# Depthwise convolution of q and k on TensorE: tiles of 64x64 replaced by tiles of 32x32, and another layout of the spilled q and k

## The chip, the core and the metric

The kernel runs on one NeuronCore of a Trainium2 chip. The metric is device time in microseconds (us) of one execution, given as the median of several runs. The core has a matrix engine (TensorE, "PE" in the profile, with its weight loads shown apart as "PEld"), a vector engine (VectorE, "DVE"), a scalar engine (ScalarE, "ACT"), GpSimd ("POOL"), and SyncE ("SP"), which here only issues DMA transfers. All arrays are float32 in this part of the kernel.

## The reference, cut to what matters

The input is x of shape (4, 192, 128, 128). Layer 0 is a channel attention; layer 1 is a dilated neighbourhood attention that takes its result and that the change does not touch.

```python
# layer 0, with 8 heads of ch = 24 channels
qkv = dwconv3x3(conv1x1(x, w_qkv), w_dw)          # 4*192 channels, 3x3 depthwise, zero padding
q, k, v, l = jnp.split(qkv, 4, axis=1)
q, k, v = (heads(q), heads(k), heads(v))          # (4, 8, 24, 128*128)
q = q / jnp.maximum(jnp.linalg.norm(q, axis=-1, keepdims=True), EPS)
k = k / jnp.maximum(jnp.linalg.norm(k, axis=-1, keepdims=True), EPS)
attn = jnp.einsum('bhcn,bhdn->bhcd', q, k) * temperature[None]
attn = softmax(attn, axis=-1)                     # only 24x24 for each head and image
out = jnp.einsum('bhcd,bhdn->bhcn', attn, v)
out = conv1x1(L + out + x, w_proj) + L            # L: a gate from the pooled l
```

So q and k, 192 channels each, are needed only for a 24x24 product and for the sums of their squares.

## The kernel before, in words

The kernel has three stages, which follow one another with some overlap.

**project** (about 0 to 820 us) computes the 1x1 convolution in 64 steps of four image rows, two images at a time. The columns for q and k, not yet convolved, are copied from PSUM by ScalarE (line 438) and written to a DRAM scratch tensor `qk_dram` by `qk_store` (lines 440 to 445, on SP's queue). Its shape is `[2 * C, H, B, W]`: by channel, then row, then image. One channel is 256 KiB in one piece. v is convolved in this stage on VectorE, ScalarE and GpSimd.

**channel_attention** (about 817 to 1598 us; line 657) runs over 8 heads. For each head, `convolved` runs once for q and once for k. It works in groups of four channels:

- SP loads a tile `u` (128 partitions, each holding image rows; 4 buffers) by four transfers of 64 partitions each (line 696), and two band matrices for each of two channels into `band` (line 693; 3 buffers).
- The 128 image rows of a channel are two strips of 64. The 3x3 convolution is a matrix product over rows: for each horizontal tap dx, a 64x64 band matrix holds the three vertical taps, and the shift in dx is a shift of the columns of the moving operand. Two channels share the 64x64 quarters of the array: channel e of the pair and strip r use the partitions `(r + e) % 2 * 64`. These are the matmuls of line 714.
- GpSimd copies the band from one half of the partitions to the other (line 701) and zeroes one of its columns (line 704).
- ScalarE copies the finished 128x512 channel from PSUM into `full` (tile name `conv`, line 723), and VectorE takes its statistics with four bn_stats (line 727), from PSUM but for the first set.

A band in a strip of 64 rows cuts off the taps across the strip border. What is missing in the two rows at the border (63 and 64), is computed by `cut_rows` (line 740): four rows, 24 channels each, are loaded (line 748), multiplied by `cuttaps` (tile `pcut`, line 756), copied (line 768), transposed on TensorE (line 771) and added: to the squares on VectorE and, as four small matmuls (line 801), to the product. For this to be sound, one column of each band is zeroed, so that the border rows get nothing from the strips.

`products` (line 781) is the 24x24 product for four images: 128 matmuls with a contraction over 128 rows, `gram` (line 786), followed by small sums (lines 801 to 818). `finish` (line 825) does the norm, softmax and the mix with the projection in pieces; `step()` runs one piece after each group of four channels.

The order on each engine in this stage is chosen by the framework's own scheduler, which may let TensorE run ahead into the next head's convolution while VectorE ends the small sums. In the other two stages the order is written out by the class `Schedule`.

**second_pass** (from about 1598 us) is layer 1.

A tensor in the trace takes its name from the variable; a float32 matmul shows as two MATMUL and two LDWEIGHTS instructions.

Of the kernel before, what the change touches and what calls it, by code (L numbers as in the profile page):

```python
# [7 lines left out]
F32 = mybir.dt.float32  # L8
# [23 lines left out]
QR = 28  # L32

# [280 lines left out]
def channel_attention_then_dilated_attention(ctx: ExitStack, tc: tile.TileContext, d, out: bass.AP):  # L314
# [16 lines left out]
    qk_dram = dram.tile([2 * C, H, B, W], F32, tag="qk_dram", name="qk_dram")  # L331
# [5 lines left out]
    with ExitStack() as early:  # L337
        band_p, u_p = (early.enter_context(tc.tile_pool(name=n, bufs=k)) for n, k in (("pab", 3), ("pau", 4)))
# [50 lines left out]
def plan_projection(nc, stage, x, wx, wx2, dwv, vboth, ring, sums, qk_dram, v_dram, v2_dram):  # L389
# [50 lines left out]
    def qk_store(n, mt):  # L440
        im0, rows = place(n)
        nc.sync.dma_start(
            qk_dram[mt * 128 : (mt + 1) * 128, rows, im0 : im0 + 2, :].rearrange("c h b w -> c h (b w)"),
            tiles.pop(("us", n, mt)).rearrange("p h b w -> p h (b w)"),
        )
# [211 lines left out]
def channel_attention(tc, d, load, qk_dram, mix1, mix2, band_p, u_p, gates):  # L657
# [7 lines left out]
    with ExitStack() as ctx:  # L665
# [3 lines left out]
        cut_p = ctx.enter_context(tc.tile_pool(name="pac", bufs=1))  # L669
        st = ctx.enter_context(tc.tile_pool(name="pas", bufs=1))  # L670
# [4 lines left out]

        logits = fin.tile([CH0, B, HEADS0, CH0], F32, tag="logits", name="logits")
        nq = fin.tile([CH0, B, HEADS0], F32, tag="nq", name="nq")
        nk = fin.tile([CH0, B, HEADS0, CH0], F32, tag="nk", name="nk")
        half = CH0 // 2

# [3 lines left out]
        def convolved(hd, which, pool):  # L684
            c0 = which * C + hd * CH0
            full = pool.tile([128, B, W // 4, CH0, 4], F32, tag="conv", name=f"conv{which}_{hd}")
            stats = st.tile([128, B, CH0, 6], F32, tag=f"stats{which}", name=f"stats{which}_{hd}")
            for c2 in range(0, half, 2):
                band = band_p.tile([128, 2, 2, 3, G], F32, tag="band", name=f"band{which}_{hd}_{c2}")
                u = u_p.tile([128, 2, 2, B * W], F32, tag="u", name=f"u{which}_{hd}_{c2}")  # L690
                for e in range(2):
                    first = c0 + e * half + c2
                    nc.sync.dma_start(band[HALVES[e], e], d["bands"][:, first : first + 2])
                    for r in range(2):
                        to = (r + e) % 2 * G
                        nc.sync.dma_start(
                            u[to : to + G, e],
                            qk_dram[first : first + 2, r * G : (r + 1) * G].rearrange("c h b w -> h c (b w)"),
                        )
                for e in range(2):  # L700
                    nc.gpsimd.tensor_copy(band[HALVES[1 - e], e], band[HALVES[e], e])  # L701
                    for r in range(2):
                        cut = G - 1 - r * (G - 1)
                        nc.gpsimd.memset(band[HALVES[(r + e) % 2], e, :, :, cut : cut + 1], 0.0)
                for c in range(2):
                    pcs = [
                        ps_c.tile([128, B, W], F32, tag="pc", name=f"pc{which}_{hd}_{c2}_{c}_{e}") for e in range(2)
                    ]
                    for dx in (1, 0, 2):
                        to, of = shifted(dx)  # L710
                        for e in range(2):
                            for r in range(2):
                                at = slice((r + e) % 2 * G, (r + e) % 2 * G + G)
                                nc.tensor.matmul(  # L714
                                    pcs[e][r * G : (r + 1) * G, :, to],
                                    band[at, e, c, dx, :],
                                    u[at, e, c, :].rearrange("p (b w) -> p b w", w=W)[:, :, of],
                                    start=dx == 1,
                                    stop=dx == 2,
                                )  # L720
                    for e in range(2):
                        ch = e * half + c2 + c
                        nc.scalar.copy(full[:, :, :, ch, :], pcs[e].rearrange("p b (v w) -> p b v w", w=4))  # L723
                        for b in range(B):

                            of = pcs[e][:, b, :] if hd or which else full[:, b, :, ch, :]
                            nc.vector.bn_stats(stats[:, b, ch, :], of)  # L727
                step()

            flat = stats.rearrange("p b c s -> p (b c) s")  # L730
            sq = st.tile([128, B, CH0], F32, tag=f"sq{which}", name=f"sq{which}_{hd}")
            sqf = sq.rearrange("p b c -> p (b c)")
            nc.vector.tensor_mul(flat[:, :, 1:5:3], flat[:, :, 1:5:3], flat[:, :, 1:5:3])
            nc.vector.tensor_add(sqf, flat[:, :, 1], flat[:, :, 4])
            nc.vector.tensor_scalar_mul(sqf, sqf, float(W // 2))
            nc.vector.tensor_add(sqf, sqf, flat[:, :, 2])
            nc.vector.tensor_add(sqf, sqf, flat[:, :, 5])
            return full, sq

        def cut_rows(hd, sums):  # L740


            pcut = ps_c.tile([128, B, W], F32, tag="pc", name=f"pcut{hd}")
            for which in range(2):
                c0 = which * C + hd * CH0
                u = cut_p.tile([4 * CH0, B * W], F32, tag=f"u{which}", name=f"cut{which}_{hd}")
                for r in range(4):
                    nc.sync.dma_start(
                        u[r * CH0 : (r + 1) * CH0],
                        qk_dram[c0 : c0 + CH0, G - 2 + r].rearrange("c b w -> c (b w)"),  # L750
                    )
                taps = cut_p.tile([4 * CH0, 3, 2 * CH0], F32, tag=f"taps{which}", name=f"cuttaps{which}_{hd}")
                nc.sync.dma_start(taps, d["cuttaps"][:, which * HEADS0 + hd])
                for dx in (1, 0, 2):
                    to, of = shifted(dx)
                    nc.tensor.matmul(
                        pcut[which * G : which * G + 2 * CH0, :, to],
                        taps[:, dx, :],
                        u.rearrange("p (b w) -> p b w", w=W)[:, :, of],
                        start=dx == 1,  # L760
                        stop=dx == 2,
                    )
            s_cut = cut_p.tile([128, B, W], F32, tag="s_cut", name=f"s_cut{hd}")
            if hd == 0:
                nc.gpsimd.memset(s_cut, 0.0)
# [3 lines left out]
            turned = ps_c.tile([128, B, 128], F32, tag="pc", name=f"turned{hd}")  # L769
            for b in range(B):  # L770
                nc.tensor.transpose(turned[:, b, :], s_cut[:, b, :], ident)
            cut = cut_p.tile([128, B, 2, G], F32, tag="cut", name=f"cutT{hd}")
            nc.scalar.copy(cut.rearrange("p b k c -> p b (k c)"), turned)
            square = cut_p.tile([128, B, 2, G], F32, tag="square", name=f"square{hd}")
# [4 lines left out]
            return cut  # L779

        def products(hd, q, sq, k, sk, cut):
            gram = ps_g.tile([HALF, B, HALF], F32, tag="gram", name=f"gram{hd}")
            for b in range(B):
                for v in range(W // 4):
                    four = lambda a: a[:, b, v].rearrange("p c w -> p (c w)")
                    nc.tensor.matmul(gram[:, b, :], four(q), four(k), start=v == 0, stop=v == W // 4 - 1)  # L786

            kept = st.tile([HALF, B, CH0, 4], F32, tag="kept", name=f"kept{hd}")
# [11 lines left out]
            for b in range(B):  # L800
                nc.tensor.matmul(extra[:, b, :], cut[:, b, 0, :two], cut[:, b, 1, :two], start=True, stop=True)
# [23 lines left out]
        def finish(hd):  # L825
# [22 lines left out]
            mixed = fin.tile([CH0, B, C], F32, tag="mixed", name=f"mixed{hd}")  # L848
            low = min(max(128 - hd * CH0, 0), CH0)
            for b in range(0, B, 2):  # L850
                pm = ps_g.tile([HALF, B, HALF], F32, tag="gram", name=f"pm{hd}_{b}")
# [3 lines left out]
                nc.vector.tensor_copy(mixed[:, b : b + 2, :], two)  # L855
            for b in range(B):
                if low:
                    nc.sync.dma_start(mix1[b][hd * CH0 : hd * CH0 + low], mixed[:low, b, :])
                if low < CH0:
                    at = G + hd * CH0 + low - 128  # L860
                    nc.sync.dma_start(mix2[b][at : at + CH0 - low], mixed[low:, b, :])
# [10 lines left out]
        for hd in range(HEADS0):  # L872
            q, sq = convolved(hd, 0, q_p)
            if hd == 0:
                same, same_row, fold, fold_rows, ones, ident, wph, tempr = (
                    load(wts, n) for n in "same same_row fold fold_rows ones ident wph temp".split()
                )
            k, sk = convolved(hd, 1, k_p)
            products(hd, q, sq, k, sk, cut_rows(hd, (sq, sk)))
            pending.append(finish(hd))  # L880
        while pending:
            step()
# [540 lines left out]
def _laid_out(inputs):  # L1423
# [33 lines left out]
    bands = np.zeros((G, 2 * C, 3, G), dw.dtype)  # L1457
    taps = dw[: 2 * C].reshape(2 * C, 3, 3)
    cuttaps = np.zeros((4, CH0, 2 * HEADS0, 3, 2, CH0), dw.dtype)
    for dy in range(3):  # L1460
        o = np.arange(max(0, 1 - dy), min(G, G + 1 - dy))
# [59 lines left out]
```

## Time and profile before

| | |
|---|---|
| time, median of 3 runs | 4362.7 us (4361.42 to 4363.07) |
| profiled execution, its span | 4359.7 us |
| profiled execution, its own time | not given apart from the span; the median lies 3.0 us above the span |
| channel attention, from the first conv matmul to the hand-over to layer 1 | 816.9 to 1598.2 us |
| one head in the middle of that stage | 960.36 to 1053.30 us: 92.94 us |
| busy in that head | PE 92.94, DVE 51.20, ACT 31.31, POOL 17.05 us; DMA 0.78, 171 GB/s |
| first head, 842 to 907 us | PE 64.93 of 65.00 us; DMA 0.96, 214 GB/s |

"Busy" is the time in which at least one instruction of the engine ran. The DMA share is the mean over the 16 DMA engines. The chain of waits is the list of work that ended last, followed back from the end; in the channel attention it runs almost wholly over TensorE. Matmul records overlap: the mean duration of one says how long it was in the array, not how often one starts.

### The profile page before, as it was taken

The page shows a single profiled execution, that of the slowest core. Times are in us where ns is not written, and L with a number is a line of the kernel's source. Part 1 is how long each engine was busy: PE and PEld are TensorE (multiplying, and loading weights), DVE is VectorE, ACT ScalarE, POOL GpSimd, SP SyncE. Part 2 cuts the span into 40 slices and gives each one's busy share as a digit, 9 for nine tenths or more (in the row PEclk, how much of TensorE's full clock was granted, in tenths as well). Part 3 has the DMA queues.
Part 4 walks back from the last instruction along what each step waited for, and adds up shares of the span by engine and source line. Part 5 has one row for each costly group of instructions (what it writes and reads, how often), then busy time and mean ns, then how long its engine had stood idle before and what let it go on. Part 6 is the DMA issues. An engine that isn't in the chain of part 4 may idle for free.

```text
span 4359.7 us, 64790 instructions
## 1 busy us (share of the span) xinstructions
PE 4248.5 (97%) x20736; PEld 1639.7 (38%) x20736; DVE 3805.5 (87%) x5492; ACT 2602.5 (60%) x4858; POOL 3316.0 (76%) x3407
## 2 busy tenths in 40 slices
PE   8999999899999989999999999999999999999996
PEld 3333333344554543333333333333333333333321
DVE  6999999855545547999999999999999999999996
ACT  6999999633323347565655655656656566566531
POOL 5888888611111114999999999999999999999998
PEclk9999999999999999999999999999999999999997
DMA  8887898778867757666666666656566566565521
GB/s 261 266 269 251 271 280 269 205 171 177 178 145 161 171 118 157 134 129 129 134 124 131 135 125 130 134 122 136 124 130 129 129 134 127 128 135 124 115 53 32
DMA packets 507362, 684.14 MB, mean 157 GB/s; under 512 B 139584, under 2 KB 321292, under 8 KB 507024
## 3 DMA queue, kind: packets, MB, share of 16 engines
q1 hardware_dynamic: 469136, 513.27, 44.9%
q0 software_dynamic: 37888, 166.74, 21.1%
q8 instruction: 167, 2.74, 0.3%
q14 instruction: 171, 1.40, 0.1%
HBM read 286.04 MB, written 201.33 MB: 112 GB/s over the span
## 4 chain that ended last, share of the span: by engine, by line
PE 78%; DVE 14%; issue 4%; POOL 2%; DMA 1%; ACT 1%; SPq 0%; DVEq 0%; POOLq 0%; ACTq 0%
PE pc L714 12%; PE sc L1179 9%; PE ex L1301 8%; PE ph L946 7%; PE pu L413 7%; PE pkv L1100 5%; DVE term L1307 4%; PE gram L786 4%; PE pkv L1103 4%; PE q L1160 4%; PE q L1157 4%; PE pu L418 3%; DVE prod L1168 3%; PE pu L564 2%; PE po L1323 2%
## 5 line engine op out<-in xcount | busy, mean ns | idle before, releaser
L1310 POOL TENSOR_TENSOR acc<-acc,term 128x512 f32<-128x512 f32 x1536 | 2035.8, 1331 | 132.1 <-DVE term L1307 45.1
L1307 DVE TENSOR_TENSOR term<-ex,vring 128x512 f32<-128x512 f32 (+2 forms) x1596 | 996.9, 660 | 55.4 <-PE ex L1301 40.6
L1168 DVE TENSOR_TENSOR prod<-q,kring 128x1536 f32<-128x1536 f32 (+1 forms) x600 | 1005.3, 1684 | 15.9 <-PE q L1157 7.7
L490 POOL TENSOR_TENSOR v_True<-v_True,side 128x512 f32<-128x512 f32 (+1 forms) x512 | 643.8, 1270 | 128.9 <-ACT side L479 99.1
L467 DVE SCALAR_TENSOR_TENSOR pa<-vboth,dwv,pa 128x1024 f32<-128x1024 f32 (+1 forms) x448 | 574.3, 1282 | 39.3 <-ACT pa L460 12.9
L1301 PE MATMUL ex<-e_sb,spread 108*128 108x512 bf16 x1728 | 567.5, 387 | 37.0 <-DVE term L1307 31.3
L701 POOL COPY band<-band 64x384 f32<-64x384 f32 x192 | 96.4, 502 | 569.8 <-DMA band<-in_bands 413.2
L714 PE MATMUL pc<-u,band 64*64 64x508 f32 (+1 forms) x4608 | 523.1, 592 | 3.1 <-ACT vboth L449 2.2
L1113 ACT COPY kring<-pkv 64x512 f32<-64x512 f32 x384 | 223.5, 582 | 417.9 <-PE pkv L1103 412.4
L998 DVE SCALAR_TENSOR_TENSOR pa<-hboth,posw,pa 128x1024 f32<-128x1024 f32 (+1 forms) x320 | 407.8, 1274 | 38.0 <-ACT pa L986 19.1
L1179 PE MATMUL sc<-prod,pick 128*32 128x512 f32 x3456 | 428.5, 598 | 1.8 <-DVE prod L1168 1.8
L727 DVE BATCH_NORM_STATS2 stats<-pc 128x6 f32<-128x128 f32 x1440 | 303.3, 283 | 141.0 <-ACT conv L723 140.7
L723 ACT COPY conv<-pc 128x512 f32<-128x512 f32 x384 | 211.5, 587 | 300.5 <-PE pc L714 288.1
L1301 PEld LDWEIGHTS <-spread 108*128 108x128 bf16 x1728 | 133.3, 97 | 647.0 <-issue 628.6
L1100 PE MATMUL pkv<-y,wkv 128*128 128x512 f32 x768 | 364.5, 596 | 10.7 <-DMA y<-moved 10.5
L413 PE MATMUL pu<-xt,wx 128*128 128x512 f32 x768 | 358.4, 610 | 16.6 <-ACT vboth L449 8.6
L946 PE MATMUL ph<-xv,mix 128*64 128x512 f32 (+1 forms) x1024 | 373.5, 594 | 0.5 <-DMA mix<-mixed 0.5
L479 ACT ACTIVATE side<-ring,dwv 128x512 f32<-128x512 f32 (+1 forms) x512 | 347.7, 723 | 27.2 <-POOL v_True L490 23.2
L1326 ACT COPY o<-po 128x512 f32<-128x512 f32 x192 | 106.3, 588 | 430.9 <-PE po L1323 227.0
L1030 ACT ACTIVATE side<-hring,posw 128x512 f32<-128x512 f32 (+1 forms) x512 | 340.9, 710 | 7.8 <-DMA side<-side 5.8
L714 PEld LDWEIGHTS pc<-u,band 64*64 64x64 f32 x4608 | 186.7, 134 | 311.2 <-issue 292.0
L1113 ACT COPY vring<-pkv 64x512 f32<-64x512 f32 x384 | 224.1, 584 | 46.1 <-PE pkv L1103 32.8
(167 smaller groups left out, 6052.7 us busy)
## 6 DMA issues: line engine op xcount, KB each, us to landing
qk_dram<-us SPq DMA_DIRECT2D x192, 512.0 KB
u<-qk_dram SPq DMA_DIRECT2D x384, 256.0 KB
side<-side POOLq DMA_DIRECT2D x124, 768.0 KB, 6.9
xt<-in_x SPq DMA_DIRECT2D x64, 512.0 KB
v_dram<-v_False SPq DMA_DIRECT2D x64, 512.0 KB
xv<-in_x SPq DMA_DIRECT2D x128, 256.0 KB
xv<-v_dram SPq DMA_DIRECT2D x128, 256.0 KB
y<-moved POOLq DMA_DIRECT2D x64, 512.0 KB, 5.2
```

The lines of the kernel that those rows point to most:

```text
L413: mm(pu, wx[:, mt * 128 : (mt + 1) * 128], tiles["xt", n][:, im, :], start=True, stop=False)
L467: nc.vector.scalar_tensor_tensor(by_row(to[:, o : o + length]), by_row(vboth[:, at : at + length, :, t % 3 : t % 3 + W]), dwv[:, 0, t : t ...
L490: nc.gpsimd.tensor_add(v[:, rows, :], v[:, rows, :], z[:, rows, :])
L714: nc.tensor.matmul(pcs[e][r * G : (r + 1) * G, :, to], band[at, e, c, dx, :], u[at, e, c, :].rearrange("p (b w) -> p b w", w=W)[:, :, of], ...
L946: mm(to, w[:, cols], tiles["xv", n, j, im], start=j == 0, stop=j == 2)
L1100: mm(rows3(tile_of("pc", key)), w, tiles["y", n, im], start=True, stop=False)
L1113: nc.scalar.copy(rows[HALVES[im], :, pad : pad + W], rows3(tiles["pkv", n, pair, im])[HALVES[e]])
L1168: nc.vector.tensor_mul(to[:, :, px].rearrange("p t (r w) -> p t r w", w=W), q.unsqueeze(1).to_broadcast([128, 3, *q.shape[1:]]), three,)
L1179: mm(sc[quad * 32 : (quad + 1) * 32, :], pick[:, QR - 4 * row : QR - 4 * row + 32], tiles["prod", n, k // NT, k % NT // 3][:, k % 3, :], s ...
L1301: mm(rows3(tile_of("ex", ("ex", n, g, t))), spread[:, t, :], e_sb, start=True, stop=True)
L1307: nc.vector.tensor_mul(rows3(to[:, px]), rows3(ex[:, px]), win)
L1310: nc.gpsimd.tensor_add(tiles["acc", n, g], tiles["acc", n, g], tiles.pop(("term", n, g, t)))
```

## The change

The strips are 32 rows high instead of 64, so there are four of them, and four channels share the array: channel e and strip r use the partitions `(r + e) % 4 * 32`. A channel now needs 4 strips times 3 taps of 32x32 matmuls. A group is eight channels, with a `u` tile of twice the size and 2 buffers instead of 4; the bands are 32x32, loaded once into `few` (32 partitions, one buffer) and copied by GpSimd into all four strips of one of two fixed `band` tiles, in twelve copies for a group. There are three inner borders (after rows 31, 63, 95), each with its own cut convolution. `qk_dram` becomes `[H, 2 * C, B, W]`: by row, then channel. bn_stats always reads `full`. On TensorE the order in this stage is now the program's own: channels are interleaved by the key `0.75 * n + k`.

```diff
-    qk_dram = dram.tile([2 * C, H, B, W], F32, tag="qk_dram", name="qk_dram")
+    qk_dram = dram.tile([H, 2 * C, B, W], F32, tag="qk_dram", name="qk_dram")
...
-        band_p, u_p = (... for n, k in (("pab", 3), ("pau", 4)))
+        band_p, u_p = (... for n, k in (("pab", 1), ("pau", 2)))
...
-            qk_dram[mt * 128 : (mt + 1) * 128, rows, im0 : im0 + 2, :].rearrange("c h b w -> c h (b w)"),
+            qk_dram[rows, mt * 128 : (mt + 1) * 128, im0 : im0 + 2, :].rearrange("h c b w -> c h (b w)"),
...
+        bands = [band_p.tile([128, 4, 2, 3, STRIP], F32, tag=f"band{k}", name=f"band{k}") for k in range(2)]
+        for band in bands:
+            nc.gpsimd.memset(band, 0.0)
...
+        def loaded(hd, which, j):
+            c0 = which * C + hd * CH0 + j
+            few = few_p.tile([STRIP, 4, 2, 3, STRIP], F32, tag="few", name=f"few{which}_{hd}_{j}")
+            nc.sync.dma_start(few..., d["bands"]...)
+            u = u_p.tile([128, 4, 2, B * W], F32, tag="u", name=f"u{which}_{hd}_{j}")
+            for e in range(4):
+                turn = e * STRIP
+                for to, of in ((slice(turn, 128), slice(0, 128 - turn)), (slice(0, turn), slice(128 - turn, 128))):
+                    if of.start == of.stop:
+                        continue
+                    first = c0 + e * (CH0 // 4)
+                    nc.sync.dma_start(
+                        u[to, e].rearrange("p c w -> p (c w)"),
+                        qk_dram[of, first : first + 2].rearrange("h c b w -> h (c b w)"),
+                    )
+            band = bands[(3 * (2 * hd + which) + j // 2) % 2]
+            for i in range(4):
+                group = slice(i * STRIP, (i + 1) * STRIP)
+                nc.gpsimd.tensor_copy(band[group, :, :, :, 1 : STRIP - 1], few[:, :, :, :, 1 : STRIP - 1])
+                for e, m in ((i, 0), ((i + 1) % 4, STRIP - 1)):
+                    nc.gpsimd.tensor_copy(band[group, e, :, :, m : m + 1], few[:, e, :, :, m : m + 1])
+            return band, u
+
+        def convolve(band, u, e, c, pc, dx):
+            to, of = shifted(dx)
+            for r in range(4):
+                at = slice((r + e) % 4 * STRIP, (r + e) % 4 * STRIP + STRIP)
+                nc.tensor.matmul(
+                    pc[r * STRIP : (r + 1) * STRIP, :, to],
+                    band[at, e, c, dx, :],
+                    u[at, e, c, :].rearrange("p (b w) -> p b w", w=W)[:, :, of],
+                    start=dx == 1,
+                    stop=dx == 2,
+                )
...
             for b in range(B):
                 for v in range(W // 4):
                     ...
                     nc.tensor.matmul(gram[:, b, :], four(q), four(k), start=v == 0, stop=v == W // 4 - 1)
+                if b == 0:
+                    cuts.append(cut_turned(hd, 2, s_cut))
+                    for edge, cut in enumerate(cuts):
+                        cut_squares(hd, edge, cut, (sq, sk))
...
             for b in range(B):
-                nc.tensor.matmul(extra[:, b, :], cut[:, b, 0, :two], cut[:, b, 1, :two], start=True, stop=True)
+                for edge, cut in enumerate(cuts):
+                    nc.tensor.matmul(
+                        extra[:, b, :], cut[:, b, 0], cut[:, b, 1], start=edge == 0, stop=edge == 2
+                    )
...
+        def head(hd):
+            ...
+            order = sorted((0.75 * n + k, n, dx) for n in range(2 * CH0) for k, dx in enumerate((1, 0, 2)))
+            for _, n, dx in order:
+                which, j, e = n // CH0, n % CH0 // 4, n % 4
+                if dx == 1:
+                    if n % 8 == 0:
+                        sources[n // 8] = loaded(hd, which, j)
+                    if n in (12, 28, 44):
+                        edge = len(us)
+                        taps = taps or cut_taps(hd)
+                        us.append(cut_loaded(hd, edge))
+                    pcs[n] = ps_c.tile([128, B, W], F32, tag="pc", name=f"pc{hd}_{n}")
+                convolve(*sources[n // 8], e, j % 2, pcs[n], dx)
+                if dx != 2:
+                    continue
+                evicted(fulls[which], stats[which], e * (CH0 // 4) + j, pcs.pop(n))
+                if n % 4 == 3:
+                    step()
+                if n in (14, 30, 46):
+                    s_cuts.append(cut_convolved(hd, len(s_cuts), us[len(s_cuts)], taps))
+                if n in (18, 34):
+                    cuts.append(cut_turned(hd, len(cuts), s_cuts[len(cuts)]))
+                ...
+            products(hd, fulls[0], sums[0], fulls[1], sums[1], cuts, s_cuts[2])
             pending.append(finish(hd))
...
+        with tc.manual_schedule(engines={mybir.EngineType.PE}):
+            for hd in range(HEADS0):
+                head(hd)
+            while pending:
+                step()
```

In `finish`, the result of the mix goes through a tile of half the size, used twice, with one empty step more. `cut_convolved` alternates between q and k from tap to tap, where before all taps of q came first. The transposes and the copies of a cut are as before, but three times for each head.

## The prediction

> **What bounds the kernel now.** I began with the page's groups, to see what one instruction of each kind lasts.
>
> ```profile
> L701 POOL COPY band<-band 64x384 f32<-64x384 f32 x192 | 96.4, 502 | 569.8 <-DMA band<-in_bands 413.2
> L714 PE MATMUL pc<-u,band 64*64 64x508 f32 (+1 forms) x4608 | 523.1, 592 | 3.1 <-ACT vboth L449 2.2
> L727 DVE BATCH_NORM_STATS2 stats<-pc 128x6 f32<-128x128 f32 x1440 | 303.3, 283 | 141.0 <-ACT conv L723 140.7
> L723 ACT COPY conv<-pc 128x512 f32<-128x512 f32 x384 | 211.5, 587 | 300.5 <-PE pc L714 288.1
> ```
>
> TensorE is never idle ahead of L714 (3.1 us in all); VectorE and ScalarE wait. Next, the chain of waits in the stage, in order of time.
>
> ```profile
> 1006.21 20.57 PE gram L786 x242
> 1029.31 20.64 PE pc L714 x165
> 1053.30 40.28 PE pc L714 x374
> ```
>
> One head is 92.94 us, all TensorE. From the chain within it: convolution 1.01 + 20.64 + 1.85 + 40.28 = 63.8, gram 1.36 + 20.57 = 21.9, pcut 3.6, turned 0.6, small sums 1.5, pm 1.5. The convolution starts 576 instructions, one per 110.7 ns. Last, the windows of one stretch of convolution and of two loads at the start of the kernel.
>
> ```profile
> 1053.30:1093.60 40.30, 40.30 (x376) 14.49 (x376) 27.34 (x126) 16.11 (x30) 9.87 (x42) 1.00 1.02 218
> ...
> 2.50:3.30 0.80, 0.00 (x0) 0.00 (x0) 0.00 (x0) 0.00 (x0) 0.00 (x0) 1.00 1.03 383
> 4.30:5.20 0.90, 0.00 (x0) 0.00 (x0) 0.00 (x0) 0.00 (x0) 0.00 (x0) 1.00 0.71 198
> ```
>
> The last two columns are DMA share and GB/s. While TensorE convolves, DMA is full too, at 218 GB/s: SP issues one group of four channels each 5.4 us, for 5.1 us of matmuls. So TensorE has the lead by little, and **DMA is the second wall right behind it**. Transfers into 128 partitions (2.50) reach 383 GB/s, transfers into 64 (4.30) 198; those of u go into 64. Last, the queue of SP in the stage:
>
> ```profile
> SPq L693 <- PE pc L714: 198.2, 64, 21.8
> ```
>
> SP waits for buffers that matmuls still read: the depth of u and band sets when loads start.
>
> **What the Trainium skill says.** "TensorE: Matmul & The Clock Gate", Part 3 (measured speedup): sixteen 32x32 matmuls ran 10.6 times as fast as one after another. This trace shows only four at once, at full rate: 4 in 425 ns (509 columns, two passes each, at the granted clock 1.00). "SBUF — State Buffer", Door 1: 64 partitions in one half reach only half of the DMA ports; 383 against 198 GB/s agrees. "DMA: Bandwidth & Descriptors", latency and other measured facts: a row pitch of 512 KiB in HBM cost little (207 of 214 GB/s), 4 MiB halved the rate. The new read has a pitch of 384 * 2 KiB = 768 KiB; the trace has no such read. The first page, Part 1: after about 3.4 us of idle TensorE runs at half clock; the trace agrees (mean 0.90 in 1600 to 1650 us, 40.75 busy).
>
> **The change, part by part, for one head.**
>
> *Convolution on TensorE.* 48 channels x 12 matmuls x 2 = 1152 instructions instead of 576, sixteen in the array instead of four: 63.8 x 2 / 4 = 31.9 us. Bounds: 30.5 (425 / 16 each), and 63.8 if only eight run at once. I take 31.9: each tile sees the same 425 ns, and the key 0.75 n + k gives the four diagonals work in turn. Weight loads (133 ns, hidden today) double in number and shrink; they stay hidden.
>
> *Cuts.* Three for one: pcut 3 x 3.6, turned 3 x 0.6, together +8.4 us; alternation of q and k may give back up to 1 us for each cut. Twelve products (24 instructions) instead of four (8): +1.0. VectorE: two more squares and eight more adds, 2 x 0.6 + 8 x 0.25 = 3.2 us; ScalarE: four more copies of 0.58 and two of 0.59. Both hidden, see below.
>
> *Program order on TensorE.* The scheduler's fill between gram and the small sums (1.0 us of convolution) becomes a wait for VectorE (0.55 + 0.53 us for kept and part, then own): +1.5. Matmuls of finish and gate stand in line, too; the empty step gives VectorE time; 0 to 2 us, I take 0.
>
> So TensorE has 31.9 + 10.8 + 1.8 + 21.9 + 4.0 + 1.5 = **72 us of work a head**, 21 less than now.
>
> *The others.* ScalarE: 48 x 0.587 + 6 x 0.58 + 3 x 0.59 + table loads = 37 us; 8 channels take it 4.7 us. VectorE: 51.2 + 3.2 = 54. Both fit in 72. PSUM: a bank is used 2.6 us by matmuls and 0.9 by the copy; six banks at 0.66 us a channel give 4.0. Tight, no wait. bn_stats from `full` frees PSUM earlier: nothing on the path.
>
> *DMA.* u is the same 12.6 MB, cuts 1.2 instead of 0.4, bands 0.6 instead of 2.4: 14.4 MB. Now rows of 4 KiB go into 128, 96 + 32, 64 + 64 and 32 + 96 partitions. At 383 GB/s for 128 and about 225 for each half (256 KiB in 1.15 us, from 5.4 us a group), a group of eight channels takes 1.34 + 4 x 1.15 + 2 x 0.58 = 7.1 us, against 10.9 now; few adds 0.46 and a cut's eight transfers 2.8 for every second group. Ends: 5.5 us if pieces in different halves overlap fully; 11 to 14 if 768 KiB costs a third to a half.
>
> *The refill loop: what is late next.* There are only two u and two bands, and one few. Let the last matmul that reads group g end at 0. Then SP may issue u for g+2 and GpSimd may copy its band. GpSimd: four copies of 720 elements and eight of 24. From 499 ns for 384 elements and 203 ns for 8 (its copy into xcol) I work out about 0.8 and 0.2: 4.9 us (3.2 to 7). The first matmul of g+2 comes at 5; TensorE interleaves, so group g+1 ends 2 us later, at 7. SP issues few for g+3 only when the copies of g+2 are done; it lands behind the seven transfers of g+2: about 1.3 + 7.1 + 0.5 + 0.7 = 9.6. (A small transfer takes 2.0 us in all, that of mix at 1596.18.) The next copies end at 14.5, group g+2 at 16.6, and so on: the starts lie 9.6, 7.6 and 9.0 us apart. With the cuts' 1.4 us a group and the rows of the last two channels arriving later, I take **10.5 us a group where TensorE needs 5.3**.
>
> During gram (22 us) both buffers fill. So a head is: group 0 in 5.3, group 1 in 7 (a cut), three groups at 10.5, the last about 10.5 + 3.6 for the cut and 2 for the tail, and 24 for gram and small sums: 5.3 + 7 + 31.5 + 16 + 24 = **83.8 us**. Idle pieces of up to 4 us may drop the clock; I leave that in the range. Gain: 92.9 - 83.8 = 9.1 us, for seven heads 64 us.
>
> *First head.* Its convolution is bound by DMA today (0.96 in 842 to 907). It starts with ScalarE free of the projection's tail, at 840, and needs 70 us of convolution with the same sum and with gate's matmuls: no gain, -5 to +10.
>
> *project.* Stores of q and k are still runs of 1 KiB, with 2 KiB instead of 256 KiB between channels; the stage's bound is TensorE (200.00 of 200.00 us in 400 to 600), which hides DMA at 0.85: nothing, at most 5 us either way. GpSimd no longer runs the first band copies there; two memsets come in: nothing.
>
> *The end.* The second half of mixed waits for the transfer of the first (2.0 us), which only later images need: 0 to 3.
>
> **Sum.** 4359.7 - 64 = 4295.7 for the profiled execution, with the last item +2 and the first head -3; the median lies 3 us above. I write 4294.
>
> **Rivals.**
>
> A, *TensorE stays the bound* (0.22): the pieces overlap in DMA, GpSimd's copies are nearer 3 us, and the loop is hidden. Head 72 to 74: gain 7 x 20 = 140, so 4223 us. For it: DMA then needs about 40 us of 72. Against: two buffers, released only at the end.
>
> B, *the new read of q and k is slow* (0.17; ends slower): strips of 4 KiB, 768 KiB apart. If a group's transfers take 11 us instead of 7.1, period and head grow: three to four groups at 13.5 to 14 bring the head to 94, the point of no gain; at 14 us (150 GB/s) the head is about 109, 7 x 16 = 112 us slower: 4475. For it: the layout before was contiguous; against: the skill's 512 KiB.
>
> C, *the array doesn't hold sixteen* (0.09): with eight at once the convolution is 63.8 us again and the cuts come on top: head 102 to 104, so 4430.
>
> My forecast, the refill loop, has 0.52, with head times from 79 to 92: 4240 to 4355 as its own range.
>
> **Numbers.** About 0.2% (9 us) is what a measurement of this kernel can tell from no change. Forecast and A give nearly all of faster, 0.73; B and C are slower but for their mild ends: 0.21; 0.06 stays for no change. The range reaches from A's end with some gain in the first head (4200) to mild forms of B (4390); outside are the rest of B and C and a few hundredths below.
>
> **What the profile will show.** Right: 9216 matmuls at L714's successor in bursts, one per 27 ns where nothing waits; a head near 84 us with TensorE idle inside the convolution for some 15 us, those waits ending with GpSimd's band copy or DMA of u; DMA near 280 GB/s or more in those stretches; gram unchanged. Wrong: no idle and a head near 72 (A); DMA share near 1 at less than 200 GB/s (B); one matmul per 50 ns with no wait (C). A clock under 0.9 in the stage would say that idle pieces cost more than I allow.

## The result, and the profile after

| | before | after |
|---|---|---|
| median, in the same session | 4362.26 us (4 runs) | 4343.31 us (4338.63 to 4350.1, 4 runs) |
| span of the profiled execution | 4359.7 us | 4348.2 us (its run took 4350.1 us, the longest of the four) |
| a head, from gram to gram | 92.95 us | 90.75 us (635.26 us for seven, 89.07 to 94.63 each) |
| first gram of the stage | 911.28 us | 910.18 us |

The ratio is 0.9956, with an interval of 0.9942 to 0.997: 19 us less, where the prediction said 68. The groups of the page of after (line, engine, operation, output and inputs, count; busy us and mean ns of one; idle time ahead of them and what ended most of it):

```profile
L712 POOL COPY band<-few 32x6 f32<-32x6 f32 x384 | 78.3, 207 | 448.9 <-DMA few<-in_bands 217.6
L720 PE MATMUL pc<-u,band 32*32 32x508 f32 (+1 forms) x9216 | 408.2, 611 | 50.1 <-DMA u<-qk_dram 28.8
L731 DVE BATCH_NORM_STATS2 stats<-conv 128x6 f32<-128x128 f32 x1536 | 313.9, 274 | 129.8 <-ACT conv L729 122.7
L729 ACT COPY conv<-pc 128x512 f32<-128x512 f32 x384 | 218.6, 586 | 199.2 <-PE pc L720 187.1
```

There are twice as many matmuls of the convolution, and the idle time ahead of them, 3.1 us before, is 50.1, 28.8 of it ended by a transfer of u. That still understates it, since a matmul that is in the array counts as busy. The chain of waits of after, in order of time (start, length, what), through one head, with most of the short pieces left out:

```profile
1004.81 5.68 PE gram L807 x64
1010.92 16.32 PE gram L807 x192
...
1030.03 8.50 PE pc L720 x225
...
1041.28 8.72 DMA u<-qk_dram
...
1050.89 7.43 DMA u<-qk_dram
...
1058.34 0.50 SPq L759
...
1058.95 2.23 DMA few<-in_bands
...
1063.38 0.83 POOL band L710
...
1064.26 0.78 POOL band L710
...
1065.09 3.63 PE pc L720 x22
1068.72 3.42 PE pcut L772 x12
1072.14 0.27 SPq L759
...
1073.73 0.35 SPq L703
...
1076.83 8.24 DMA u<-qk_dram
...
1085.11 5.17 PE pc L720 x127
1090.28 2.75 PE pcut L772 x12
```

Before, the whole of a head was TensorE's own work. Now 24.4 us of it are transfers of u (line 703), one behind another, with few and the copies of the band in turn. At 1068.72 the chain runs from pcut over SP's queue at 759, the loads of the cut rows, to the next u: SP waited there for pcut, and the transfers of u stood behind.

The windows of after, before and in the waits for u (window, its length; busy us and instructions of TensorE, its weight loads, VectorE, ScalarE, GpSimd; granted clock, DMA share, GB/s):

```profile
1034.00:1036.00 2.00, 2.00 (x81) 1.50 (x63) 2.00 (x12) 1.37 (x4) 0.19 (x1) 1.00 0.03 8
...
1040.00:1042.00 2.00, 2.00 (x77) 1.30 (x50) 2.00 (x12) 1.56 (x4) 1.54 (x4) 1.00 1.04 363
1042.00:1044.00 2.00, 1.91 (x39) 0.41 (x28) 2.00 (x11) 0.94 (x3) 0.00 (x0) 1.00 1.04 236
1044.00:1046.00 2.00, 2.00 (x12) 0.52 (x8) 1.65 (x9) 0.54 (x1) 0.00 (x0) 1.00 1.01 229
...
1068.00:1070.00 2.00, 2.00 (x14) 0.45 (x6) 1.46 (x8) 0.59 (x1) 0.00 (x0) 0.50 0.89 236
...
1082.00:1084.00 2.00, 2.00 (x26) 0.34 (x22) 0.88 (x4) 0.54 (x1) 0.00 (x0) 1.00 0.98 188
```

A count in brackets is of the instructions that ran at some time of the window, so for matmuls it includes those that were in the array when the window began; a weight load, one for each matmul, lasts only about 0.1 us, and its count is nearly that of the starts. From 1034 to 1036 and from 1082 to 1084 TensorE works on the convolution alone and is "busy" for 2.00 us, but with 81 matmuls and 63 weight loads in the first window and 26 and 22 in the second, in which the chain above stands on a transfer of u. The 12 matmuls of 1044 to 1046 are something else: they belong to pcut, whose 12 take 2.75 us one after another, with or without a refill. DMA is full in most windows from 1040 on. It moves 363 GB/s in the 2 us in which most of the piece of 128 partitions is in flight, and then 229 to 236 in the two windows with the smaller pieces, hardly more than the 218 of before. From 1068 to 1070 the granted clock was 0.50. The queue of SP in the whole stage (what waited, for what; us, times, longest):

```profile
SPq L703 <- PE pc L720: 163.9, 17, 23.6
SPq L759 <- PE pcut L772: 65.4, 16, 6.3
```

The first line is the release of u. The second is new: 65 us in which SP issues nothing.

### The profile page after: what moved, and what is told of

The parts are those of the page before. It is cut to its first block, busy times and chain, and to the rows that moved or that the text cites. A ratio compares the mean times of both kernels' runs of the same rounds, so it can differ in the third digit from the quotient of the medians.

```text
span 4348.2 us, 74751 instructions
## 1 busy us (share of the span) xinstructions
PE 4178.9 (96%) x25728; PEld 1655.8 (38%) x25728; DVE 3833.7 (88%) x5572; ACT 2633.4 (61%) x4906; POOL 3411.2 (78%) x3409
## 4 chain that ended last, share of the span: by engine, by line
PE 69%; DVE 13%; DMA 5%; POOL 5%; issue 4%; ACT 2%; SPq 1%; POOLq 0%; DVEq 0%; ACTq 0%
PE sc L1239 9%; PE ex L1361 8%; PE ph L1006 7%; PE pu L414 7%; PE pkv L1160 5%; DVE term L1367 4%; PE pc L720 4%; PE gram L807 4%; PE pkv L1163 4%; PE pu L419 3%; PE q L1217 3%; PE q L1220 3%; DMA u<-qk_dram 3%; DVE prod L1228 3%; POOL acc L1370 3%
## 5 line engine op out<-in xcount | busy, mean ns | idle before, releaser
L1228 DVE TENSOR_TENSOR prod<-q,kring 128x1536 f32<-128x1536 f32 (+1 forms) x600 | 1003.9, 1681 | 19.4 <-PE q L1217 10.1
L720 PE MATMUL pc<-u,band 32*32 32x508 f32 (+1 forms) x9216 | 408.2, 611 | 50.1 <-DMA u<-qk_dram 28.8
L712 POOL COPY band<-few 32x6 f32<-32x6 f32 x384 | 78.3, 207 | 448.9 <-DMA few<-in_bands 217.6
L731 DVE BATCH_NORM_STATS2 stats<-conv 128x6 f32<-128x128 f32 x1536 | 313.9, 274 | 129.8 <-ACT conv L729 122.7
L1160 PE MATMUL pkv<-y,wkv 128*128 128x512 f32 x768 | 364.3, 596 | 10.7 <-DMA y<-moved 10.5
L480 ACT ACTIVATE side<-ring,dwv 128x512 f32<-128x512 f32 (+1 forms) x512 | 347.7, 724 | 31.4 <-POOL v_True L491 27.7
L720 PEld LDWEIGHTS pc<-u,band 32*32 32x32 f32 x9216 | 183.8, 104 | 236.4 <-issue 79.6
```

Source lines behind the costliest of these rows:

```text
L720: nc.tensor.matmul(pc[r * STRIP : (r + 1) * STRIP, :, to], band[at, e, c, dx, :], u[at, e, c, :].rearrange("p (b w) -> p b w", w=W)[:, :, of],
L1160: mm(rows3(tile_of("pc", key)), w, tiles["y", n, im], start=True, stop=False)
L1228: nc.vector.tensor_mul(to[:, :, px].rearrange("p t (r w) -> p t r w", w=W), q.unsqueeze(1).to_broadcast([128, 3, *q.shape[1:]]), three,)
```

## The experiments

The questions were: what makes the refill loop longer than forecast (the layout, the transfers' form, the bands, the cuts' loads, the late release of u), what keeps the convolution on TensorE above 31.9 us even without it, and whether the written order has a part. Each edit is to the kernel after, but for the first. A ratio is to before, run again in the same session; the medians of before lie between 4362.26 and 4363.99 us over the sessions. Differences from after are between medians, and since the four executions of after spread over 11.5 us, a few microseconds can't be told from nothing. "A head" is from gram to gram in the profile, the mean of those available; it belongs to one execution, which for after was the longest of four.

**The layout alone**

```diff
 # before.py, with the qk_dram, store and loads of the new layout only
+    qk_dram = dram.tile([H, 2 * C, B, W], F32, tag="qk_dram", name="qk_dram")
```

> The kernel before, with qk_dram laid out by row, then channel, and nothing else (tiles of 64x64, four u, three bands). Its u transfers read 4 KiB in one piece at a pitch of 768 KiB, into 64 partitions. Theory 1 (the layout costs nothing; the rate of u is set by how many partitions a transfer reaches): 4350 to 4372 us, DMA in a stretch of convolution still 215 to 235 GB/s. Rival (the pitch of 768 KiB slows the read, rival B of the prediction): a group's transfers grow by a fifth or more and the head with them, 4450 us or more, below 190 GB/s.

Measured: 4362.05 against 4363.15 us, ratio 0.9997 (0.9988 to 1.0005), heads of 92.95 us. Neither the stores nor the reads with a pitch of 768 KiB cost anything that can be told, with DMA as full as it was (0.99 at 223 GB/s from 1047 to 1087 us). Rival B is out.

**No refill**

```diff
+            g = 3 * (2 * hd + which) + j // 2
+            if g >= 2:
+                return kept[g % 2]
```

u, few and band are loaded for the first two groups only, so all later groups convolve stale rows.

> The changed kernel; u, few and the band copies are done only for the first two groups of eight channels, and all later groups use these two again (so q and k of later heads are wrong; the load is left out). Theory 1 (waiting for the refill of u and band makes the head 90 us instead of the 72 of TensorE's own work): head 72 to 76 us, 4205 to 4240 us. Rival (TensorE's order, with its waits for ScalarE and the cuts, sets the head): head 85 us or more, 4305 us or more.

Measured: 4241.47 us, ratio 0.9723 (0.9709 to 0.9738), a head 76.37, each just above the range. The chain of waits of this kernel through one head:

```profile
1002.62 13.41 PE pc L726 x354
1016.03 2.70 PE pcut L778 x12
1018.73 3.35 PE pc L726 x89
1022.08 0.59 PE turned L796 x4
...
1023.82 9.04 PE pc L726 x199
...
1039.50 9.61 PE pc L726 x264
...
1053.77 5.68 PE gram L813 x64
```

It is TensorE again but for 1.9 us before gram, in which ScalarE copies the last cut and the last channel. So the refill is what bounds after, and costs 90.75 - 76.37 = 14.4 us a head in these two profiles (102 us between the medians, of which the first gram, 9.2 us earlier here, is a part); but even without it a head takes 76.4, not 72. The pieces of convolution sum to 39.8 us, with two of 1.04 and 3.35 that are not shown: 34.5 ns an instruction.

**Bands once**: few and its copies for the first two groups only, so later bands are stale.

```diff
+            if g < 2:
                 few = ...; nc.sync.dma_start(few..., d["bands"]...)
-            for i in range(4):
+            for i in range(4 if g < 2 else 0):
```

> The changed kernel; few and the twelve copies on GpSimd are done only for the first two groups (later bands are wrong), u is loaded as before. Theory 1a (the rate and the late issue of u set the refill): 5 to 20 us less, 4322 to 4338 us. Theory 1b (the copies of the band, behind few, set it, as the prediction's loop had it): 40 to 70 us less, 4273 to 4303 us.

Measured: 4321.34 us, ratio 0.9906 (0.9891 to 0.9921), a head 87.3: 22 us less than after. GpSimd's part of the loop, with the load of few, is real, and a minority of it.

**Whole rows**: u unturned, four transfers of all 128 partitions (the strips then lie in the wrong partitions).

```diff
-                for to, of in ((slice(turn, 128), slice(0, 128 - turn)), (slice(0, turn), slice(128 - turn, 128))):
+                for to, of in ((slice(0, 128), slice(0, 128)),):
```

> The changed kernel; the rows of u are not turned: one transfer into all 128 partitions for each e, four for a group instead of seven (strips are then in the wrong partitions; the bytes are the same). Theory 1a (pieces that reach half of the ports, and seven issues on SP, make the transfers 8 to 9 us for a group instead of 5.5): DMA 330 GB/s or more while it loads, head 78 to 83 us, 4255 to 4295 us. Rival (the read from DRAM at this pitch sets the rate): below 260 GB/s, 4330 us or more.

Measured: 4306.71 us, ratio 0.988 (0.9863 to 0.9896), a head 85.1: 37 us less, for the same bytes, which is less than Theory 1a had. A window in the refill of this kernel:

```profile
1038.00:1042.00 4.00, 4.00 (x119) 2.76 (x125) 3.90 (x17) 2.33 (x5) 2.73 (x5) 1.00 1.01 390
```

390 GB/s against 229 to 236: the same DMA engines, as full as in after, move two thirds more when a transfer covers all the partitions. This is the best of the windows; the two others of 4 us with a share over 0.9 (1062 to 1070) have 317 and 329. The edit also makes four issues on SP out of seven, so the 37 us are the price of the pieces together with their issues.

**The cuts' loads from ScalarE's queue**

```diff
-                    nc.sync.dma_start(
+                    nc.scalar.dma_start(      # in cut_loaded
```

> The changed kernel with the loads of the cuts' rows issued from ScalarE's queue instead of SP's. In the changed kernel these loads wait on SP for the matmuls of the cut before (65 us in the stage), and the transfers of u stand behind them in the same queue. Theory 1c (this head-of-line wait is a good part of the refill): 20 to 45 us less than the changed kernel, 4298 to 4323 us. Rival (u is late for its buffer or its transfer time alone): within 8 us of it, 4335 to 4350 us.

Measured: 4355.73 us, ratio 0.998 (0.9974 to 0.9987): 12 us slower than after. SP waits for pcut only at line 748 any more (19.0 us from 860 to 1500), but ScalarE now waits for the rows of the cuts, and its copies stand behind those waits. The waits of this kernel's ScalarE:

```profile
ACT conv L729 <- DMA cut<-qk_dram: 19.1, 17, 3.7
...
ACT cutT L792 <- DMA cut<-qk_dram: 19.4, 3, 7.0
```

The move put the blockage onto an engine that TensorE needs, and both the theory and its rival missed; the run says nothing on what the wait cost SP. The run with the cuts' loads left out, below, was made for that.

**few from GpSimd's queue**

```diff
-            nc.sync.dma_start(
+            nc.gpsimd.dma_start(      # few, in loaded
```

> The changed kernel with the load of few issued from GpSimd's queue. There it does not stand behind the seven transfers of u, and SP does not wait for the copies. Theory 1b (the wait for few behind u, 218 us on GpSimd in the stage, is the part of the refill that leaving out the bands took away, 22 us): 10 to 22 us less than the changed kernel, 4321 to 4333 us. Rival (the twelve copies themselves): no gain, 4338 to 4350 us.

Measured: 4333.42 us, ratio 0.9932 (0.9917 to 0.9947): 10 us less than after. In the profiles its heads, 89.5 us, are 1.2 shorter each, and the first gram starts at 904.61 instead of 910.18. That start alone proves little: it is 911.28 in before and 905.06 in the layout alone, at equal medians.

**u in four tiles**, of two channels each, two buffers of each: the same memory, but a quarter is free once its own matmuls have read it.

```diff
-            u = u_p.tile([128, 4, 2, B * W], F32, tag="u", ...)
+            u = []
             for e in range(4):
+                u.append(u_p.tile([128, 2, B * W], F32, tag=f"u{e}", ...))
...                                         # loads and matmuls take u[e] accordingly
```

> The changed kernel with u as four tiles of two channels each, with two buffers each, in the same memory: the part of each channel pair is free for refill when its own matmuls have ended, up to 2 us before the group's last. Theory (the late release of the whole tile is part of the loop): 10 to 20 us less than the changed kernel, 4323 to 4333 us. Rival (transfers are back to back anyway): within 6 us, 4337 to 4349 us.

Measured: 4318.31 us, ratio 0.9899 (0.9884 to 0.9914), a head 85.7: 25 us less than after, more than was expected. The queue of SP in this kernel shows the release in quarters, 65 waits instead of 17:

```profile
SPq L704 <- PE pc L721: 178.3, 65, 20.9
```

The wait for pcut is not among the nine longest of SP any more.

**A shorter eviction**: no refill, and ScalarE copies one image of four from the second head on (the rest of `full` is stale).

```diff
+            some = slice(0, B) if hd == 0 else slice(0, 1)
...                                         # and the edit of no refill; one full for q and one for k
-            nc.scalar.copy(full[:, :, :, ch, :], pc...)
+            nc.scalar.copy(full[:, some, :, ch, :], pc...[:, some])
```

> The kernel without refill, in which from the second head on ScalarE copies only one image of four out of PSUM (q and k of later heads are wrong; three quarters of the copy left out, one tile of full for all heads). Its head is 76.4 us, of which 39.9 are convolution where the prediction had 31.9. Theory 2a (copies and six PSUM banks hold TensorE back): the convolution falls to 32 to 34 us, the head to 69 to 71 us, 4190 to 4205 us. Theory 2b (TensorE itself does not start more than one matmul per 34 ns in this order): no change, 4235 to 4247 us.

Measured: 4254.92 us, ratio 0.9754 (0.9738 to 0.977), a head 76.05 against 76.37; the pieces of convolution are the same to 0.01 us (13.41, 3.35, 9.04, 9.62). So the length of ScalarE's copies does not hold the convolution. That it is 13 us slower in all than no refill comes from the start: its first gram begins at 921.61 instead of 901.03. The cause of that stays open.

**Quarters of u and few from GpSimd together**: the edits of both.

> The changed kernel with both: u as four tiles of two channels (two buffers each), and few issued from GpSimd's queue. Alone they gave 25 and 10 us. Theory (they act at different places of the loop: release of u, and the band's load behind u): 4303 to 4313 us. Rival (the same wait, taken away twice): 4315 to 4322 us.

Measured: 4309.47 us, ratio 0.9877 (0.9863 to 0.9892): 53 us less than before, 34 less than after, and the fastest version here that leaves nothing out. Its heads, 86.5 us, are not shorter than with the quarters alone (one of them took 90.2). Its first gram starts at 905.29 instead of 917.25; that this is what few adds is not shown, as that start also varies by itself.

**The cuts' rows loaded once**: later heads use the rows of the first.

```diff
-            us = []
+            if cut_kept:
+                return cut_kept
+            us = cut_kept
```

> The changed kernel; the rows of the cuts are loaded once for the whole kernel (later cuts use them again, and are wrong; 185 of 192 transfers left out), so that neither their wait on SP nor their bytes stand ahead of u. Theory 1c (the wait of the cuts' loads on SP holds u back): 20 to 40 us less than the changed kernel, 4303 to 4323 us; issued from ScalarE they held ScalarE back instead, which hid that. Rival (the cuts' loads do not matter): 4335 to 4348 us.

Measured: 4322.12 us, ratio 0.9908 (0.9891 to 0.9924), a head 86.3: 21 us less than after, with pcut still run. The loads of the cuts, 1.2 MB a head out of 14.4, cost some 3 us a head where they stand, ahead of u in SP's queue (21 us over seven heads). The two profiles differ by 4.5 a head, but this one is of the shortest of its four executions (4309.89 us), and that of after of the longest. This run takes away their bytes and their wait together; SP's 65 us of waits for pcut speak for the wait, but the bytes alone would be 5 us a head at 230 GB/s if nothing hid them. How much is which stays open.

**Quarters, few from GpSimd, and whole rows** (strips in the wrong partitions as above).

> As ube_few, and the rows of u not turned: one transfer into 128 partitions for each e (strips in the wrong partitions). Theory 1 (with transfers at 380 GB/s, early release and few on its own queue the loop is nearly hidden): the head near 78 us, 4255 to 4270 us, against 4241 us without any refill. Rival (what is left is TensorE's order or the cuts' loads): 4285 us or more.

Measured: 4263.91 us, ratio 0.9774 (0.976 to 0.9789), a head 80.7. The head is longer than was expected, the total in its range. The three edits together leave 4.3 us of the 14.4 that the refill costs.

**TensorE's order left to the scheduler**

```diff
-        with tc.manual_schedule(engines={mybir.EngineType.PE}):
+        with ExitStack():
```

> The changed kernel with TensorE's order in the channel attention left to the framework's scheduler, as before the change, and nothing else. Theory (the written order costs only the wait after gram and the stalls in line, 1 to 2 us a head, and gains the interleaving): 0 to 40 us slower than the changed kernel, 4343 to 4385 us, with fewer matmuls in the array at once. Rival (the written order, stalling in line for u, costs much of the expected gain): 4325 us or less.

Measured: 4351.56 us, ratio 0.9971 (0.9961 to 0.998), a head 91.1: some 8 us slower than after, at the edge of what the runs of both can tell (4334.78 to 4359.63 here). Leaving the order to the scheduler gains nothing, so the written order is not what loses the time.

**No refill and no cuts** (cuts of the first head used for all), one run:

> The kernel without refill, in which the cut convolutions and their transposes are left out from the second head on (its cuts are those of the first head, so later heads are wrong). Its head without refill is 76.4 us, with 9.3 us of cuts' matmuls and 1.9 us of waiting for the last cut's copy. Theory 3a (the array drains and fills again at each change of shape, which is most of the 8 us by which the convolution is over 31.9): head 58 to 61 us. Theory 3b (the shape changes cost little; a matmul each 34 ns is the rate in this order): head 64 to 66 us.

Measured: 4166.86 us, a head 64.62. The chain of waits and a window of this kernel:

```profile
997.44 20.48 PE pc L726 x538
...
1018.09 17.10 PE pc L726 x422
```

```profile
1000.00:1010.00 10.00, 10.00 (x332) 7.69 (x317) 9.55 (x50) 7.35 (x14) 0.00 (x0) 1.00 0.02 5
```

The convolution takes 37.6 us when nothing else stands in it, 2.2 less than with the cuts between. In the middle there are 317 weight loads in 10 us, one per 31.5 ns (the 332 matmuls include those that were in the array at 1000), so 36.3 us for 1152; the other 1.3 us are left for its ends, where the first and the last channels have the array to themselves. So interruptions by the cuts are the smaller part of the excess over 31.9, and the larger part is the rate itself.

**No refill, and the channels in fours**, without the stagger, one run:

```diff
-            order = sorted((0.75 * n + k, n, dx) ...)
+            order = sorted((n // 4 * 3 + k, n, dx) ...)
```

> The kernel without refill, with the order of TensorE by groups of four channels: tap by tap for the four channels e = 0 to 3, so that all sixteen tiles work on the same tap and width, and four channels end at once. Theory 3c (mixed widths in the written order cost the rate): the convolution falls from 39.9 to 33 to 36 us, head 70 to 73 us. Rival (four banks are freed at once and the next four channels wait for ScalarE's copies): head 78 to 85 us.

Measured: 4268.56 us, a head 79.18 against 76.37, so 2.8 us more. The stagger of 0.75 is worth having. What mixed widths cost in the array is not shown: in this run weight loads of the convolution wait for ScalarE's copies, 39.3 us in 104 waits from 860 to 1500, as the rival had it, and these may hide a gain.

Not tried: two buffers for the rows of a cut, a third u, and whatever would tell whether the weight loads hold the stream of matmuls. They are busy for 7.69 of 10.00 us in the window above, where before they were for 14.49 of 40.30.

## Why the prediction was right or wrong

**Right: the mechanism.** TensorE lost its place as the bound of the stage to the loop of buffers, SP, DMA and GpSimd; the waits inside the convolution end with u and with the band; gram is unchanged (22.0 us). The head gained 2.2 us instead of 9.1. One sign looked different from the forecast: TensorE counts as busy for 85.77 of the 90.13 us of the head from 1004.81, so the loss shows as fewer matmuls and not as 15 us of idle time.

**Right: what costs nothing.** The layout (0.9997) and its pitch of 768 KiB, where the Trainium skill's "DMA: Bandwidth & Descriptors", latency and other measured facts, has a small loss at 512 KiB and half the rate at 4 MiB; the evictions; the first head (gram 1.1 us earlier). The hand-over came 18.8 us earlier (mix issued for layer 1 at 1577.36 instead of 1596.18), with the 2 us of the second transfer of mixed inside. The profiled execution then lost 7 us in layer 1, which the change doesn't touch and where the run without refill lost 3.4.

**Right: GpSimd.** Twelve copies in 4.9 us. In one head of after, the copies of its six groups are busy for 19.3 (line 710) + 10.1 (line 712) = 29.4 us, 4.9 a group.

**Wrong: the period of the refill loop, 10.5 us a group; 12.0 measured.** This is the step of the sum that failed. The order of the matmuls on TensorE is the program's, so the first one of each group can be found by counting: it is number 1, 169, 361, 553, 745 and 937 of a head's 1152. In the trace of after, the head from 1004.81 divides like this:

| part of the head | forecast | measured |
|---|---|---|
| gram and small sums | 24 us | 25.2 us |
| group 0 | 5.3 us | 5.7 us |
| group 1 | 7 us | 7.0 us |
| groups 2, 3 and 4 | 31.5 us | 12.7 + 9.7 + 13.2 = 35.6 us |
| group 5, the last cut and the tail | 16 us | 16.6 us |
| head | 83.8 us | 90.1 us |

On the mean of seven heads groups 2 to 4 take 36.1 us, 12.0 each, which is 4.6 of the 7.0 us that a head is over the forecast. Without refill the same three groups take 27.3. Three terms behind the period were too small, as follows; how the 4.6 us divide over them is not shown.

**First term: 31.9 us of convolution; 39.8 measured without refill.** I took one matmul per 27.7 ns. The runs show 31.5 in an undisturbed stretch, 1.3 us at the ends and 2.2 around the cuts; the forecast had the last two as free. What holds the stream at 31.5 stays open. The cuts themselves were smaller than I allowed: 8.15 us of pcut instead of 10.8, small sums 2.8 instead of 4.0, pm 0.1 instead of 1.5; the wait of gram for the last copies, 1.9 us, was not in the 72. So the floor of a head is 76.4 us, +4.4. Rival A's 4223 was thus out of reach with any refill; without one at all the kernel takes 4241.

**Second term: 7.1 us for a group's u; 9.1 at the measured 229 GB/s** (2.1 MB; an estimate). I let the piece of 128 partitions run at 383 GB/s and took 1.15 us for each piece of 96 or 64. In the chain shown, SP begins to issue a group at 1073.73 and the last of its transfers has landed at 1085.07: 11.3 us, where the loop had 1.3 + 7.1 and 0.7 to the end. The forecast of 280 GB/s or more came true only for the first piece of a group (363 in 1040 to 1042). One of the readings behind it was weak as well: the window of 198 GB/s had a DMA share of 0.71, so DMA was not full in it. The Trainium skill's "SBUF — State Buffer", Door 1, makes the ports reached depend on the partitions of a transfer. The cost of the form, with its issues, is shown: whole rows give up to 390 GB/s and 37 us. Why the pieces don't reach that together is only argued: SP issues the two parts of a channel one after the other, and a part of 64 or 32 reaches only half of the ports.

**Third term: 1.4 us a group for the loads of the cuts.** I counted their bytes and not their place. They share one tile of `cut_p`, so each load waits for the pcut before it, and SP issues in order: u stands behind. Removing them, bytes and wait together, gave 21 us.

**The sum.** Against the run without refill, the refill is 14.4 us instead of 11.8 and the floor 4.4 higher, together 90.75 - 83.8 = 7.0 a head. That is bookkeeping: in a loop, a slower TensorE and a slower refill don't simply add. That 7 times 7.0 is just 4343 - 4294 is partly luck: the forecast's own sum gives 4295.7 + 2 - 3 and 3 more for the median, 4297.7 and not 4294, and the heads are those of an execution 6.8 us above the median. Of the 16.6 us a head that the smaller tiles bring (92.95 - 76.37), 14.4 went into the refill. Taken away one by one, whole rows give 37, quarters of u 25, bands 22 (the other queue for few alone 10) and cuts 21 us, where the whole refill is 102; quarters and few together give 34, with whole rows 79. None is the cause alone.

**The clock** had a small part, which the prediction had left to its range. The mean is 0.98 in the head that starts at 1004.81, with 0.50 from 1068 to 1070, where pcut took 3.42 us instead of 2.75, and 0.96 to 1.00 in the seven heads; without refill it is 1.00. The missing shares, times the length of each head, come to about 11 of the 635 us, so at most 1.6 of the 14.4 us a head (an estimate).

## What to carry to other kernels

When a change makes the matmuls of a stage shorter, price the refill next as a loop: release of the buffer, place in the issuing queue, the transfer in the partitions that it covers, the copy behind it. Cut a tile that is filled ahead into the pieces in which it is read (25 us here for no memory), and don't put a load that waits for a late consumer into the queue that must run ahead. In a window of a packed matrix engine, read the counts of one kind of instruction, best of the weight loads, and not the busy time: here it was 2.00 of 2.00 us with 63 of them and with 22. And see which tile the counted ones belong to.

## What the runs showed of the hardware that I had not expected

- A 32x32 float32 matmul of 508 columns is in the array as long as a 64x64 one (611 and 592 ns on the mean), but sixteen at once are not sixteen times as fast: one starts per 31.5 ns in an undisturbed stretch, where 425 / 16 is 26.6. Within a burst most records start 16 to 17 ns apart; in the trace of before, with 64x64 tiles, 6 to 7. The Trainium skill's "TensorE: Matmul & The Clock Gate", Part 3, has about 4 ns for each tile; no run here shows that. The prediction's own citation of it, 10.6 times for sixteen, is 40 ns a matmul (425 / 10.6, an estimate); 31.5 lies between that and the ideal.
- Complementary pieces of 96 and 32 or 64 and 64 partitions, one after another in one queue, moved 229 to 236 GB/s with DMA at a share of 1.0; whole rows 317 to 390 at 0.91 to 1.01.
- A row pitch of 768 KiB in DRAM, for the reads of u, had no price that these runs can tell (0.9997).
